# A layer-norm, graph-message, convolution and gating kernel: a new clock for the planner that orders its instructions

## The chip, the cores and the metric

The kernel runs on one core of a Trainium2 chip. The core has a matrix engine (TensorE, written PE in the profile, with PEld for its weight loads), a vector engine (VectorE, DVE), an activation engine (ScalarE, ACT), a general engine (GpSimd, POOL) and a queue engine (SyncE, SP). Each works through its own list of instructions in order and waits on semaphores for the others. DMA transfers are issued from SP, POOL and ACT. The metric is the device time of one execution in microseconds (us), lower is better. A measurement of this kernel can tell a difference of about 0.3%, some 6 us.

## The reference

The input is `x`, 32 batches of 512 nodes with 256 features, and `adj`, a 512 by 512 mask for each batch; everything is fp32. With `h = relu(layernorm(x))` the output is `x + gru(...)`:

```python
xc = transpose(h); c = relu(bn1(conv1(xc, 1 tap)))
x_conv = relu(bn2(conv2(c, 17 taps)) + xc)
s = h @ w_se.T + b_se                      # 3 numbers for each node
A = exp(-|s_n - s_m|^2) * adj
x_nmp = A @ relu(h @ w_msg.T + b_msg)
x_in = concat([x_conv, x_nmp])
gi = x_in @ w_ih.T + b_ih;  gh = h @ w_hh.T + b_hh
r = sigmoid(gi_r + gh_r); z = sigmoid(gi_z + gh_z)
out = x + (1 - z) * tanh(gi_n + r * gh_n) + z * h
```

## The kernel before

**The work.** The 32 batches pass through five parts, and each part is a Python generator, called a stream, that emits instructions and now and then yields.

- `begins` (`begin`) turns a normalised batch into the layout with features on partitions (`hT`), on PE and ACT for the first 8 batches and with VectorE transposes after a trip through DRAM (`xd`) for the others, and stores it to DRAM (`hd`).
- `rows` (`all_rows`, `rows`, `conv1`) loads `hT` back (`load_row`, two buffers shared with `begins`) and makes the 1-tap convolution into `h1`, the input of the 17-tap convolution.
- `conv` (`convolution`) computes the 17-tap convolution with a scheme of transformed operands and weights: 7 groups of batches, 25 products in each. VectorE prepares the operands (`operand_some`), VectorE and ACT prepare the 25 transformed weights during group 0 (`prepare_some`), which are stored to `wd` and loaded again for later groups (`load_weights`). After a product ACT copies the PSUM banks out (`z`, `n`), VectorE sums them into `y`, and `evacuate` (L711) scales `y` on ACT into `part`, a ring of two buffers, from which POOL stores to `cd`. For the first two batches it writes `xconv` directly.
- `graphs` (`graph`) loads `hTg`, makes messages, the four small products and exponentials of the kernel matrix (`kernel_exp`), masks them (`masked`) and multiplies (`gather`). The small products use one bank of the convolution (`pair[1]`) and three banks of the pool `ps_g`.
- `gates` (`gates`, `unit`) computes the gated unit and stores to `out` with accumulating DMAs from POOL. Its large weights lie in a pool `late` that takes the room of the weight preparation's pool `prep` (`late_pools`).

**What sets the order.** The order of instructions on every engine is fixed while the program is built, by a planner with a simulated clock. `now` is PE's clock: each matmul adds its cost (`matmul`, L134). The `Engine` class (L116) keeps for VectorE and ACT the time at which each would be free. The loop at the end of the kernel takes, of the streams whose last yielded time is not after `now`, the one with the lowest pacing clock, lets it emit up to its next yield, and calls `fill()` (L1530), which runs due actions from the list `LATER`, `evacuate`, and background work (norms, operands, weights, sums) while VectorE is planned to be free within 1.5 us. The stream `rows` has the lowest pacing clock, so it goes first whenever it is ready. If no stream is ready, `now` advances by 0.25.

**The clock before.** An `Engine` operation starts at `max(self.free, now)` and takes `fixed + each * size`; it knows nothing of what its operands wait for. A consumer is held until `free + LAG`, with `LAG = 0.6`. DMAs are issued directly and their landing is a guess, such as `HR_AT[b] = now + 8.0` in `load_row` and `PARTS.append(act.free + 5.0)` in `evacuate`. PE's clock never waits for an operand or a bank. Loads enter SP's list where the planner emits them; on the chip SP waits there until the buffer is free, and whatever stands behind it waits too.

Of the kernel before, what the change touches and what calls it, by code (L numbers as in the profile page):

```python
# [50 lines left out]
def kernel(  # L51
# [43 lines left out]
    const = ctx.enter_context(tc.tile_pool(name="const", bufs=1))  # L95
    front = ctx.enter_context(tc.tile_pool(name="front", bufs=2))
    cv = ctx.enter_context(tc.tile_pool(name="cv", bufs=1))
    dram = ctx.enter_context(tc.tile_pool(name="dram", bufs=1, space=bass.MemoryType.DRAM))
    acc = ctx.enter_context(tc.tile_pool(name="acc", bufs=3, space=PSUM))
    gps = ctx.enter_context(tc.tile_pool(name="gps", bufs=3, space=PSUM))  # L100
    first_ctx = ExitStack()
    cps = first_ctx.enter_context(tc.tile_pool(name="cps", bufs=2, space=PSUM))
    ctx.enter_context(tc.manual_schedule())
    late = None

    now = 5.0
    LAG = 0.6
# [6 lines left out]

    class Engine:
        def __init__(self, engine, fixed, each):
            self.engine, self.fixed, self.each, self.free = engine, fixed, each, 0.0

        def behind(self, other):
            self.free = max(self.free, other.free + 0.1)

        def __getattr__(self, name):
            def issue(*tiles, **more):
                size = max(elements(t) for t in tiles if hasattr(t, "shape"))
                self.free = max(self.free, now) + self.fixed + self.each * size
                getattr(self.engine, name)(*tiles, **more)  # L128

            return issue  # L130

    dve, act = Engine(nc.vector, 0.12, 0.00108), Engine(nc.scalar, 0.16, 0.0009)

    def matmul(ps, lhsT, rhs, **more):  # L134
        nonlocal now
        now += max(0.223, 0.005 + elements(ps) / 600.0)
        nc.tensor.matmul(ps, lhsT, rhs, **more)  # L137

    def turn(ps, a):
        nonlocal now  # L140
        now += 0.11
        nc.tensor.transpose(ps, a, ident)  # L142

    def keep_warm(n):

        for _ in range(n):
            nc.tensor.transpose(unused[:, :P], ident, ident)
# [22 lines left out]
    def store_at(t, dst, src):  # L170
        todo = [lambda: nc.gpsimd.dma_start(dst, src)]

        def run():
            if todo:
                todo.pop()()

        STORES.append(run)
        later(t, run)
# [8 lines left out]
    ARRIVES = (0.0, 7.0, 11.0, 13.0)  # L187
# [6 lines left out]
    def fetch(b, xs=None):  # L194
        XS[b] = front.tile([P, NT, D], F32, name="x_sb", bufs=2) if xs is None else xs
        step = NT // 2 if b == 0 else NT
        for c in range(0, NT, step):
            nc.sync.dma_start(
                XS[b][:, c : c + step], x[b].rearrange("(c p) d -> p c d", p=P)[:, c : c + step]
            )  # L200

    def load(b, xs=None):
        if b not in XS:
            fetch(b, xs)
        NORMS[b] = norm(b)
        NORM_AT[b] = max(now + 7.0, 50.0) if b >= G else ARRIVES[b]

    def load_row(b):
        if b not in HR:
            settle_stores()  # L210
            HR[b] = front.tile([P, ND, N], F32, name="hT", bufs=2)
            nc.sync.dma_start(HR[b], HD[b])
            HR_AT[b] = now + 8.0

    def load_graph(b):
        if b < B and b not in HG and begun > b:
            settle_stores()
            HG[b] = front.tile([P, ND, N], F32, name="hTg", bufs=1)
            nc.sync.dma_start(HG[b], HD[b])

    def load_gates(b):
        if b >= B or b in HB:
            return
        settle_stores()
        HB[b] = late.tile([P, ND, N], F32, name="hTb", bufs=2)
        nc.sync.dma_start(HB[b], HD[b])
        HB_AT[b] = now + 8.0

    def load_conv(b):

        if b < B and b not in XC and evacuated.get(b, 1e9) <= now:
            XC[b] = late.tile([P, ND, N], F32, name="xconv", bufs=2)
            nc.sync.dma_start(XC[b], CD[b])
            XC_AT[b] = now + 7.0
# [14 lines left out]
    def load_sums(b, d):  # L249
        if b < B and (b, d) not in XN:  # L250
            settle_stores()
            XN[b, d] = late.tile([P, N], F32, name="xnb", bufs=2)
            nc.sync.dma_start(XN[b, d], ND_[b, d])
            XN_AT[b] = now + 6.0
# [3 lines left out]
    vec = const.tile([P, _NCOL], F32)  # L258
    nc.sync.dma_start(vec, vecs)
    w1 = const.tile([P, ND, D], F32)  # L260
    nc.sync.dma_start(w1, conv1_w)

    prep_ctx = ExitStack()
    prep = prep_ctx.enter_context(tc.tile_pool(name="prep", bufs=1))
    wraw = prep.tile([P, ND, 2, 3, 3, D], F32)
    nc.gpsimd.memset(wraw[:, :, 0, 0, 0, :], 0.0)
# [3 lines left out]
    wmsg = const.tile([P, ND, D + 3], F32)  # L270
    bmsg = const.tile([P, D + 3], F32)
    ident = const.tile([P, P], F32)
    make_identity(nc, ident)
    mhalf = const.tile([P, 4], F32)
    nc.gpsimd.memset(mhalf, -0.5)

    def rsqrt(dst, var):
# [4 lines left out]
        nc.gpsimd.tensor_tensor(dst, t[:, :n], mhalf[:, :n], op=ALU.pow)  # L282
# [15 lines left out]
    h1 = const.tile([P, Q * RV], F32)  # L298
# [4 lines left out]
    def zeros(g):  # L303
        at = input_of(g)
        for b in range(B + 1):
            v = U * b - STARTS[g]
            if 0 <= v <= sizes(g)[0]:
                nc.gpsimd.memset(at[:, : Q if v == sizes(g)[0] else LEAD, :, v : v + 1], 0.0)
                if v > 0:
                    nc.gpsimd.memset(at[:, Q - 1 : Q, :, v - 1 : v], 0.0)  # L310
# [3 lines left out]
    class Graphs:  # L314


        def __init__(self):
# [6 lines left out]
            nc.gpsimd.memset(self.aug, 1.0)  # L324
            nc.gpsimd.memset(self.augr, 0.0)
            nc.gpsimd.memset(self.augl, -1.0)
# [3 lines left out]
        def ask(self, more):  # L330
# [3 lines left out]
            for k in range(self.asked, min(self.asked + more, NT * B)):  # L334
# [3 lines left out]
                if b < TURNED:  # L338
                    nc.sync.dma_start(m, adj[b, c * P : (c + 1) * P, :])
                for g in range(P // 32 if b >= TURNED else 0):  # L340
                    at = c * P + 32 * g
                    nc.sync.dma_start(
# [37 lines left out]
    def norm_some(b):  # L380

        if now < NORM_AT[b]:
            return False
# [152 lines left out]
    def weights_first():  # L536
# [10 lines left out]
        for j1 in ORDER:  # L547
# [12 lines left out]
            for j2 in ORDER:  # L560
# [7 lines left out]
                for k in range(2):  # L568
# [4 lines left out]
                    nc.scalar.dma_start(WD[len(WS)][:, k], w[k])  # L573
# [4 lines left out]
    def weights_again():  # L578


        for m in range(25, 25 * NG):
            W_BASE.append(taken)
            w = {}
            for k in (1,) if m % 25 == LONE else (2, 0, 1):
                yield
                w[k] = new_w()
                if k < 2 or m >= 50:
                    nc.sync.dma_start(w[k], WD[m % 25][:, k])
            WS.append(w)
            W_AT.append(now + 7.0)  # L590
# [10 lines left out]
    def third_weight(m):  # L601
# [5 lines left out]
        later(dve.free + 0.4, lambda: nc.gpsimd.dma_start(WD[m % 25][:, 2], w[2]))  # L607
# [103 lines left out]
    def evacuate():  # L711
# [10 lines left out]
        if g == 0 and b < 2:  # L722
# [10 lines left out]
            if o == ND - 1:  # L733
                evacuated[b] = XC_AT[b] = act.free + 0.7 + LAG
# [7 lines left out]
        act.free += 0.7  # L742
        PARTS.append(act.free + 5.0)
        n0, n1 = Q * first, min(Q * last, N)
        later(act.free + 0.4, lambda: nc.gpsimd.dma_start(CD[b][:, o, n0:n1], part[:, : n1 - n0]))
        if o == ND - 1 and last == U:
            evacuated[b] = PARTS[-1]
# [34 lines left out]
    def prepare_some():  # L782
        nonlocal prepare_at
        if len(WS) >= 25 or len(WS) >= at_product + 3 or now < prepare_at:
# [4 lines left out]
    def convolution():  # L789
# [28 lines left out]
        for g in range(NG):  # L818
# [3 lines left out]
            if g == 1:  # L822
                first_ctx.close()
                cps = ctx.enter_context(tc.tile_pool(name="cps2", bufs=1, space=PSUM))
# [3 lines left out]
            for n in range(25):  # L828
# [6 lines left out]
                if late is None and len(WS) >= 25:  # L835
# [48 lines left out]
    def late_pools():  # L884
        nonlocal late, wih, whh, wsum, tsum
        prep_ctx.close()
        late = ctx.enter_context(tc.tile_pool(name="late", bufs=1))
        whh = late.tile([P, ND, 3 * D], F32, name="whh")
        wih = late.tile([P, 2 * ND, 3 * D], F32, name="wih")
        nc.sync.dma_start(whh, w_hh)  # L890
        nc.sync.dma_start(wih, w_ih)
# [80 lines left out]
    def kernel_exp(at):  # L972

        nonlocal now, bank_at, exp_waits
# [6 lines left out]
        for c in range(NT):  # L981
            k = slice(32 * c, 32 * c + 5)
            nc.tensor.matmul(  # L983
# [3 lines left out]
        now += 1.15  # L987
# [33 lines left out]
    def blocks(t, rows, o):  # L1021
        for g in range(P // 32):
            at = o * P + 32 * g
            nc.sync.dma_start(
# [11 lines left out]
    def begin(b):  # L1036
# [4 lines left out]
        if b >= TURNED:  # L1041
# [3 lines left out]
            nc.gpsimd.dma_start(XD_[b].rearrange("(c p) d -> p c d", p=P), xs)  # L1045
            yield now + 7.0
# [3 lines left out]
            yield now + 8.0  # L1050
# [8 lines left out]
            nc.gpsimd.dma_start(HD[b], HT[b])  # L1059
# [9 lines left out]
        for d in range(ND):  # L1069
            norm_t(b, d)  # L1070
# [6 lines left out]
    def rows(g, b):  # L1077
        nonlocal made, made_at
        for o in range(ND):
            conv1(g, b, o)  # L1080
# [5 lines left out]
    def graph(b):  # L1086
# [3 lines left out]
        if b == 0:  # L1090
            HG[0] = HT[0]
            yield act.free + LAG
        elif b not in HG:
            load_graph(b)
            yield now + 9.0
        msg = front.tile([P, NT, D], F32, name="msg", bufs=1)
        for c in range(NT):
            messages(b, msg, c)
            yield now
        told = b + 1  # L1100
        factors()
        yield dve.free + LAG
# [11 lines left out]
        for n in range(NT):  # L1114
            masked(b, at, n)
# [4 lines left out]
        for d in range(ND):  # L1120
            gather(b, msg, at, d)
# [4 lines left out]
    def gates(b):  # L1126
# [4 lines left out]
        if b < B - 1:  # L1131
            nc.sync.dma_start(out[b], x[b])
        else:
            nc.sync.dma_start(out[b][:, :P], x[b][:, :P])
# [3 lines left out]
        if b == 0:  # L1138
            yield now + 8.0
# [70 lines left out]
        def store(y, o, s):  # L1210
            for g in range(P // 32):
# [3 lines left out]
                if is_last(o):  # L1215
                    (nc.scalar if g % 2 else nc.sync).dma_start(dst, src)
                else:
                    nc.gpsimd.dma_start(dst, src, accum_op=ALU.add)  # L1218

        fast = FIRST_FAST <= b < B - PLAIN  # L1220
        if b == B - PLAIN:
            for w, at in ((whh, w_hh), (wih, w_ih)):
                nc.sync.dma_start(w[:, 0, D : 2 * D], at[:, 0, D : 2 * D])
# [331 lines left out]
    def all_rows():  # L1555
# [5 lines left out]
        for g in range(1, NG):  # L1561
            for b in batches(g):
# [5 lines left out]
                rows_wait = True  # L1568
                load_row(b)
                if b + 1 in batches(g) and b + 1 < begun:  # L1570
                    later(now + 2.5, lambda b=b: load_row(b + 1))
# [25 lines left out]
    unused, waits = acc.tile([P, N], F32, name="ps_acc"), 0  # L1597
    keep_warm(16)
# [7 lines left out]
    brz = const.tile([P, 2 * ND], F32)  # L1606
# [6 lines left out]
    bn = const.tile([P, ND], F32)  # L1613
# [9 lines left out]
    nc.sync.dma_start(wmsg[:, :, :D], w_msg)  # L1623
    nc.sync.dma_start(wmsg[:, :, D:], w_se)
    nc.sync.dma_start(bmsg[:, :D], b_msg.to_broadcast([P, D]))
    nc.sync.dma_start(bmsg[:, D:], b_se.rearrange("k o -> o k").to_broadcast([P, 3]))
    for c in range(ND):
        for k0, k1 in ((0, 9), (9, TAPS)):
            nc.sync.dma_start(wflat[:, c, k0 + 1 : k1 + 1, :], conv2_w[:, c, k0:k1, :])
# [78 lines left out]
```

## Time and profile before

| | |
|---|---|
| median of 3 runs | 2067.28 us (2066.85 to 2071.51) |
| profiled execution's own time | 2067.35 us |
| span of its instructions | 2065.6 us |
| PE busy | 2012.4 us, 97% of the span |
| DVE, ACT, POOL busy | 69%, 43%, 22% |
| mean granted TensorE clock | 0.989 of full |
| DMA engines, mean over slices from 0.4 to 0.98 | 183 GB/s |

The profiled execution is 0.07 us over the median, and 1.8 us of it lie outside the span. A wait row reads: engine, what it wanted to do, `<-`, what released it, then total us, how often, and the longest. In the window rows the columns are the stretch, its length, and then the busy time and the number of instructions of PE, PEld, DVE, ACT and POOL, the granted clock, the DMA share and GB/s. In a timeline row: start, duration, engine, line, operation, output and inputs, count, and in brackets the idle time of the engine before it with its releaser. Most operations stand at the line of a helper (L128, L137, L142), so that tile names tell them apart.

### The profile page before, as it was taken

What the parts mean: (1) busy time and instruction counts of PE and PEld (TensorE: products, weight loads), DVE (VectorE), ACT (ScalarE), POOL (GpSimd) and SP (SyncE); (2) the same over time, 40 slices, a digit from 0 to 9 for tenths busy, and PEclk for the clock granted to TensorE, in tenths of its full rate; (3) what the DMA queues carried; (4) which work ended last, traced back from release to release, by engine and by line L of the source; (5) the groups of instructions that cost most, each with busy time, mean ns of one, the idle gap of its engine ahead of it and who ended that gap; (6) DMA issues with size and microseconds to landing.
All of it is one profiled execution on the core that took longest, in us unless ns stands there. A gap on an engine that the chain in (4) does not pass through costs nothing. (4 is left out here: it accounts for less than half of the span.)

```text
span 2065.6 us, 27386 instructions
## 1 busy us (share of the span) xinstructions
PE 2012.4 (97%) x9199; PEld 1360.9 (66%) x9199; DVE 1416.3 (69%) x2626; ACT 888.4 (43%) x1805; POOL 451.1 (22%) x578
## 2 busy tenths in 40 slices
PE   8999889999999999999999999999999999999998
PEld 4878556676676766677577676667775677664444
DVE  6789378885878848687587775677875777752223
ACT  6554454335543445433454334554334633334221
POOL 2101022321212213122141221231221311114222
PEclk9999999999999999999999999999999999999999
DMA  7455668898979869778789788797886776756554
GB/s 286 150 174 184 225 209 196 192 226 226 223 197 203 190 192 205 201 182 212 183 193 223 172 204 206 164 197 204 207 204 175 189 158 159 173 118 143 63 92 36
DMA packets 581227, 378.70 MB, mean 183 GB/s; under 512 B 457648, under 2 KB 475344, under 8 KB 579952
## 3 DMA queue, kind: packets, MB, share of 16 engines
q1 hardware_dynamic: 419616, 279.02, 49.1%
q0 software_dynamic: 153184, 84.70, 23.9%
q10 hardware_dynamic: 8288, 13.24, 1.7%
q8 instruction: 73, 1.20, 0.2%
q14 instruction: 66, 0.54, 0.1%
HBM read 278.81 MB, written 114.56 MB: 190 GB/s over the span
## 5 line engine op out<-in xcount | busy, mean ns | idle before, releaser
L1218 POOL DMA_DIRECT2D out_dram<-o_sb x252 | 275.9, 1718 | 659.1 <-DVE o_sb L128 628.9
L137 PE MATMUL ps_acc<-xnb,wih 128*128 128x512 f32 (+1 forms) x772 | 364.4, 593 | 0.7 <-DVE ps_acc L128 0.7
L137 PEld LDWEIGHTS ps_c<-xd,w 128*128 128x128 f32 x2304 | 288.6, 191 | 55.0 <-issue 38.9
L137 PEld LDWEIGHTS ps_c<-x,w 128*128 128x128 f32 x2032 | 258.4, 193 | 72.3 <-issue 49.2
L137 PE MATMUL ps_c<-xd,w 128*128 128x135 f32 (+1 forms) x2304 | 291.8, 280 | 7.0 <-ACT ps_c L128 7.0
L137 PE MATMUL ps_c<-x,w 128*128 128x135 f32 (+2 forms) x2032 | 267.4, 281 | 11.4 <-ACT n L128 5.0
L137 PE MATMUL ps_acc<-hTb,whh 128*128 128x512 f32 (+2 forms) x580 | 239.5, 523 | 0.4 <-ACT r L128 0.4
L137 PE MATMUL ps_acc<-xconv,wih 128*128 128x512 f32 (+1 forms) x580 | 238.9, 519 | 0.3 <-DVE ps_acc L128 0.3
L137 PE MATMUL ps_g<-at,msg 128*128 128x512 f32 x512 | 227.1, 593 | 0.8 <-DVE at L128 0.8
L137 PEld LDWEIGHTS ps_acc<-xnb,wih 128*128 128x128 f32 x772 | 142.6, 191 | 115.6 <-issue 108.7
L137 PEld LDWEIGHTS ps_g<-at,msg 128*128 128x128 f32 x512 | 95.4, 190 | 106.4 <-issue 101.1
L137 PEld LDWEIGHTS ps_acc<-xconv,wih 128*128 128x128 f32 x580 | 107.6, 190 | 74.9 <-issue 67.5
L137 PEld LDWEIGHTS ps_acc<-hTb,whh 128*128 128x128 f32 x580 | 104.8, 191 | 78.6 <-issue 71.2
L128 DVE TENSOR_TENSOR msg<-ps_g,bmsg 128x256 f32<-128x256 f32 x128 | 53.7, 420 | 143.5 <-PE ps_g L137 143.1
L128 DVE SCALAR_TENSOR_TENSOR x<-x,x 128x544 f32<-128x544 f32 (+5 forms) x161 | 137.5, 854 | 2.9
L128 DVE TENSOR_TENSOR o_sb<-hTb,r 128x512 f32<-128x512 f32 x63 | 43.3, 687 | 124.1 <-ACT r L128 123.5
L128 ACT ACTIVATE ps_c<-ps_c 128x270 f32<-128x270 f32 (+1 forms) x144 | 56.1, 389 | 167.8 <-PE ps_c L137 167.8
L128 DVE TENSOR_TENSOR x<-x 128x272 f32<-128x272 f32 (+5 forms) x280 | 127.4, 497 | 0.2
L137 PE MATMUL ps_g<-hT,w 128*128 128x512 f32 (+8 forms) x296 | 122.1, 560 | 3.7 <-DMA hT<-hd 2.5
L137 PE MATMUL ps_g<-wmsg,hTg 128*128 128x259 f32 x496 | 123.5, 382 | 0.7 <-DVE aug L128 0.7
L128 ACT ACTIVATE h<-ps_g,bn_shift,bn_scale 128x252 f32<-128x252 f32 (+8 forms) x212 | 86.5, 485 | 73.2 <-PE ps_g L137 73.2
L128 DVE TENSOR_TENSOR xd<-x 128x544 f32<-128x544 f32 (+1 forms) x144 | 102.5, 716 | 14.0 <-PE ps_c L137 13.7
(149 smaller groups left out, 2927.5 us busy)
## 6 DMA issues: line engine op xcount, KB each, us to landing
w<-wd SPq DMA_DIRECT2D x414, 256.0 KB, 3.4
m_sb<-in_adj_dram SPq DMA_DIRECT2D x384, 64.0 KB, 3.8
hT<-hd SPq DMA_DIRECT2D x33, 512.0 KB, 4.4
hd<-hT POOLq DMA_DIRECT2D x32, 512.0 KB, 5.5
hTb<-hd SPq DMA_DIRECT2D x32, 512.0 KB, 4.6
xnb<-nd SPq DMA_DIRECT2D x64, 256.0 KB, 3.0
out_dram<-o_sb POOLq DMA_DIRECT2D x252, 64.0 KB, 4.9
hTg<-hd SPq DMA_DIRECT2D x31, 512.0 KB, 4.3
```

The source lines that it names most:

```text
L128: getattr(self.engine, name)(*tiles, **more)
L137: nc.tensor.matmul(ps, lhsT, rhs, **more)
L1218: nc.gpsimd.dma_start(dst, src, accum_op=ALU.add)
```

## The change

Only the planner changes; the arithmetic, the tiles, the pools' sizes and the number of matmuls of the computation stay. All instructions may come in another order.

1. **Dependencies in the clock.** Every tile's reads and writes are noted by region (`region`, `note`). An operation starts at `max(self.free, after(...))`, where `after` gives the end of the writes of its inputs and of all accesses to its output, plus `HAND = 0.04` across engines, and the release of the ring buffer under it (`BORN`). PE's `now` waits in the same way (`on_pe`).
2. **Durations.** The constants are replaced: VectorE 0.12 + 0.00108 per element becomes 0.066 + 0.00106 plus a tail of 0.085; ACT 0.16 + 0.0009 becomes 0.05 + 0.00087 plus a tail of 0.12, with a factor of 2.2 for outputs whose last step is over 8 elements and 0.1 for each bias or scale tile. `LAG` becomes 0.17.
3. **DMAs in the clock.** `sp`, `pool` and `act` issue DMAs through `Engine.dma_start`, with an issue time, 8 transfers in flight for the hardware queues and 8 for POOL's, and a common line (`FLOW`) of 1.85 us and a rate. Its result replaces the guesses: `HR_AT`, `HB_AT`, `XC_AT`, `XN_AT`, `W_AT` and `NORM_AT` become `done(...)`, and `PARTS` gets the modelled end of the store to `cd`.
4. **Loads and buffers.** `load_row` is asked for when the ring `hT` is to be free (0.5 earlier), the transposes of `begin` wait for `front.free("hT", 2)`, and the streams yield until `gps.free("ps_g")` before they take a bank.
5. **A gate on ACT.** `norm_some` and `prepare_some` return at once when ACT is planned busy for more than `BUSY = 0.5` beyond `now`. `late_pools` waits until `prep.over() <= now + 1.0`.

```diff
-    LAG = 0.6
+    LAG = 0.17
+    BUSY = 0.5
+    HAND = 0.04
...
+    def after(who, outs, ins):
+        at = 0.0
+        for a in ins:
+            for k, end in met(a.tensor.name, region(a)):
+                if k[4]:
+                    at = max(at, end if k[5] == who else end + HAND)
+        for a in outs:
+            at = max(at, BORN.get(a.tensor.name, 0.0))
+            for k, end in met(a.tensor.name, region(a)):
+                if k[5] != who:
+                    at = max(at, end + HAND)
+        return at
...
+        def free(self, name, bufs=None):
+            ring, n = self.rings.get(name, []), bufs or self.bufs
+            return released(ring[-n]) + HAND if len(ring) >= n else 0.0
...
+        def dma_start(self, dst, src, **more):
+            run = 4 * min(dst.ap[-1][1], src.ap[-1][1])
+            name = "P" if self.name == "POOL" else "H"
+            lanes = LANES.setdefault(name, [0.0] * 8)
+            at = max(self.free, after("DMA", [dst], [src]), lanes[0])
+            if name == "P":
+                issue = 1.1 if run < 512 else 0.78 if run == 1024 else 0.55
+            else:
+                issue = 0.53 if run < 512 else 0.43 if run == 1024 else 0.37
+            self.free = at + issue
+            rate = 150e3 if run < 512 else 330e3
+            flow = (self.free + 1.85, 4 * elements(dst) * dst.shape[0] / rate)
+            FLOW.append(flow)
...
+            for arrives, cost in FLOW:
+                end = max(end, arrives) + cost
+                if (arrives, cost) == flow:
+                    break
...
-                size = max(elements(t) for t in tiles if hasattr(t, "shape"))
-                self.free = max(self.free, now) + self.fixed + self.each * size
+                at = max(self.free, after(self.name, some[:1], some[1:] + given))
+                wide = some[0].ap[-1][0] > 8 and self.name == "ACT"
+                each = self.each * (2.2 if wide else 1.0)
...
+                self.free = at + fixed + each * max(elements(t) for t in some) + 0.1 * len(given)
+                note(self.name, some[:1], some[1:] + given, self.free + self.tail)
...
-    dve, act = Engine(nc.vector, 0.12, 0.00108), Engine(nc.scalar, 0.16, 0.0009)
+    dve, act = Engine("DVE", nc.vector, 0.066, 0.00106, 0.085), Engine("ACT", nc.scalar, 0.05, 0.00087, 0.12)
...
+    def on_pe(out, ins, took):
+        nonlocal now
+        now = max(now, after("PE", [out], ins)) + took
+        note("PE", [out], ins, now + 0.163)
...
-            HR_AT[b] = now + 8.0
+            HR_AT[b] = done(HR[b])
...
-        if now < NORM_AT[b]:
+        if now < NORM_AT[b] or act.free > now + BUSY:
             return False
...
-        act.free += 0.7
-        PARTS.append(act.free + 5.0)
+        PARTS.append(1e9)
+        mine = len(PARTS) - 1
...
+        def leaves():
+            PARTS[mine] = pool.dma_start(CD[b][:, o, n0:n1], part[:, : n1 - n0])
+            if o == ND - 1 and last == U:
+                evacuated[b] = PARTS[mine]
+
+        later(act.free + 0.2, leaves)
...
-        if len(WS) >= 25 or len(WS) >= at_product + 3 or now < prepare_at:
+        if len(WS) >= 25 or len(WS) >= at_product + 3 or now < prepare_at or act.free > now + BUSY:
...
-                if late is None and len(WS) >= 25:
+                if late is None and len(WS) >= 25 and prep.over() <= now + 1.0:
                     late_pools()
...
+            yield gps.free("ps_g")
             messages(b, msg, c)
...
+                yield front.free("hT", 2) - 0.5
                 load_row(b)
```

## The prediction

> **What bounds the kernel now.** I read the page's first lines, then who PE waited for, then the busy time by stretches, then the timeline at the two longest groups of pauses, and last the DMA rows.
>
> ```profile
> span 2065.6 us, 27386 instructions
> PE 2012.4 (97%) x9199; PEld 1360.9 (66%) x9199; DVE 1416.3 (69%) x2626; ACT 888.4 (43%) x1805; POOL 451.1 (22%) x578
> PEclk9999999999999999999999999999999999999999
> ```
>
> PE is the bound almost everywhere, and its work does not change. So all that a new order can win is PE's idle time, 2065.6 - 2012.4 = 53.2 us, and the time lost while its clock was lowered: the mean granted clock is 0.989, so 1.1% of 2065.6, about 23 us. At the end 6.5 us follow PE's last matmul (2059.1); 46.7 us of idle lie ahead of it. The wait rows over the whole span add up to nearly that:
>
> ```profile
> PE ps_c L137 <- ACT ps_c L128: 7.0, 5, 3.1
> PE ps_c L983 <- ACT z L128: 6.7, 3, 4.0
> PE ps_c L137 <- ACT n L128: 5.0, 5, 2.0
> PE ps_c L137 <- ACT z L128: 4.4, 3, 1.7
> PE ps_g L137 <- DMA hT<-hd: 2.5, 2, 1.2
> ```
>
> The reader is to see that PE waits for ACT, few times and long, and hardly for a load. Asked for by stretch, the waits before 280 us sum to 27.4 us and those after to 18.8 us; of the first, 5.0 lie before 30 us, the start. Where the pauses stand, the clock falls:
>
> ```profile
> 206.00:222.00 16.00, 12.37 (x43) 6.04 (x42) 9.12 (x21) 6.73 (x16) 1.30 (x1) 0.79 0.27 97
> 269.00:280.00 11.00, 6.13 (x47) 5.39 (x46) 10.59 (x16) 10.46 (x16) 2.90 (x5) 1.00 0.73 233
> 564.00:578.00 14.00, 9.19 (x45) 8.15 (x44) 13.76 (x24) 7.38 (x13) 7.38 (x9) 0.76 1.09 230
> 834.00:850.00 16.00, 11.99 (x47) 7.42 (x46) 12.05 (x18) 11.39 (x18) 6.31 (x6) 0.79 0.61 92
> ```
>
> The timeline shows two causes. First, evacuation:
>
> ```profile
> 564.35 1.37 ACT L128 ACTIVATE part<-y,bn_shift,bn_scale 128x522 f32<-128x522 f32 x1
> 567.19 1.20 PE L137 MATMUL ps_c<-x,w 128*128 128x136 f32 x8 [1.74 <-ACT z L128]
> 567.27 1.38 ACT L128 ACTIVATE part<-y,bn_shift,bn_scale 128x522 f32<-128x522 f32 x1
> 570.11 1.02 ACT L128 ACTIVATE part<-y,bn_shift,bn_scale 128x360 f32<-128x360 f32 x1 [1.45 <-DMA cd<-part]
> 570.93 0.48 ACT L128 ACTIVATE ps_c<-ps_c 128x272 f32<-128x272 f32 x1
> 571.46 0.82 PE L137 MATMUL ps_c<-xd,w 128*128 128x136 f32 x2 [3.07 <-ACT ps_c L128]
> ```
>
> At 570.11 ACT stands for 1.45 us because `part`'s old contents had not landed, and the bank copy that PE needs is queued behind. Second, the small products at 842 us:
>
> ```profile
> 837.17 4.43 ACT L128 ACTIVATE y<-z 128x1620 f32<-128x1620 f32 x3
> 841.63 0.68 ACT L128 ACTIVATE z<-ps_c 128x270 f32<-128x270 f32 x2
> 842.37 1.22 PE L983 MATMUL ps_c<-right,left 5*128 5x512 f32 x1 [4.01 <-ACT z L128]
> ```
>
> **The idle time in five heaps.** Evacuation: 2.0 + 2.9 us at 273 and 277 and 1.7 + 3.1 at 567 and 571, together 9.7. Small products behind `z`: 6.7. Loads of `hT`: 2.5. The start: 5.0. The rest of the head, 30 to 280 us: 27.4 - 5.0 - 4.9 = 17.5. The rest after 280: 18.8 - 4.8 - 6.7 - 2.5 = 4.8. The clock by slices of 52 us (0.93 is 3.6 us lost, 0.97 is 1.6): 0 to 52 us 3.6; 52 to 155 3.1; 207 to 310 7.2; 568 to 620 3.6; 826 to 878 3.6; the rest under 3.
>
> **Durations and evacuation.** The planner before gives a `part` of 522 elements 0.16 + 0.0009 x 522 + 0.7 = 1.33; the row says 1.34, so that was right. But the same shape written to `xconv` in group 0 it gives 0.61 where the row says 1.31: over four large ones 2.8 us of ACT work that it doesn't see, and PE's 4.9 us near 275 follow them. The new clock gives 0.05 + 2.2 x 0.00087 x 504 + 0.2 + tail = 1.33. For `part` the guess is the landing: act.free + 5, where the stores issued at L745 took 3.6 us in the median and up to 9.0, and POOL can be busy first with 4.4 us of output stores. ACT stood 12.7 us, 16 times, for these landings. With `PARTS` at the modelled landing, and unknown until the store is issued, `evacuate` steps aside. Of 9.7 us I take 8.4 away; the cover is that the other streams then have PE work, which 97% busy supports. The clock loss at 568 (3.6) goes with it: -12. If `part` is late next, `xconv` loads and the gates are later, but they are asked for far ahead (no PE wait for `xconv` now).
>
> **A rule on the clock.** The row: the 16 us at 206 ran at 0.79 after pauses of 2.5 and 1.1 us, with three matmuls between. [...]
>
> **The gate on ACT and the head.** Norms and weight preparation no longer pile up on ACT when it is 0.5 us behind. In the head PE waits for `n`, `z`, `w`, `right` and `augr`, single waits of up to 2.5 us, from ACT half busy and DVE 75 to 93% busy in the 52 us slices from 52 to 207. What DVE limits stays. No row shows how much of the 17.5 us is order and how much is work; the ends are 0 and 17.5, and I take half, 8.7, since DVE is idle for 17 us at 250 while PE still waits. Half of the clock loss from 52 to 310 (10.3) goes too: -5. The gate's own price is a late weight; PE's wait for `w` is 2.2 us now and `prepare_some` stays up to 3 weights ahead, which hides it. Without that cover 25 weights at 1 us each would cost 25 us. `late_pools` moved by a product or two: 24 matmuls of 0.11 each, 2.7 us, of gates' start, paid nowhere because gates' work is only put off among other PE work.
>
> **The small products.** The three copies take 4.43 us; the planner before already gives 3 x 1.62. `kernel_exp` yields for `bank_at` only when a product is open, and that is unchanged. The 6.7 us may fall elsewhere: 0, with ends -10 (its clock loss with it) and +10.
>
> **Loads and their queue.** Asking for `hT` when its buffer is free takes SP's waits at L212 (57 us for stores, 48 for conv1's matmuls) off SP; behind them stood weights, masks and the other copies of `hT`. PE hardly waited for those, so this wins the 2.5 us at most. Against it stands the missing margin: before, a row was held for 8 us after the ask; now until the modelled landing, and `rows` goes first when ready, so a late landing is a pause of PE. For 512 KB the empty line gives 0.37 + 1.85 + 1.59 = 3.81 us.
>
> ```profile
> hT<-hd SPq DMA_DIRECT2D x33, 512.0 KB, 4.4
> q1 hardware_dynamic: 419616, 279.02, 49.1%
> q0 software_dynamic: 153184, 84.70, 23.9%
> ```
>
> The median is 4.4, one in ten takes over 6.6. `FLOW` adds what was planned ahead, in one line by arrival. [...] By the row it is 0.6 at the median, 33 x 0.6 = 20 us, before `FLOW`'s own addition and the emission step (0.9 to 3.4 us of matmuls), which swallow most. I take 0.15 us each, near the row: +5. The other loads (`hTg`, `hTb`, `xnb`, weights) are asked for a stage ahead. Nor does the wait for `ps_g` add work; PE's waits for that pool's banks were a few us.
>
> **Margins.** `LAG` falls from 0.6 to 0.17 and durations lose their padding: an ACT copy of 272 is 0.05 + 0.24 + 0.12 = 0.41 against the row's 0.40; VectorE's 128x512 is 0.69 against 0.69. An error of 0.05 us now shows. With some 60 places where PE has nothing else, 3 us; ends 0 and 10.
>
> **Sum.** -12 (evacuation) - 13.7 (head) - 2.5 + 5 (loads) + 3 (margins) = -20.2. From the profiled execution's 2067.35, which is the median's 2067.28, to 2047.
>
> **Rivals.**
> *Nearly all pauses go.* The clock now sees what PE waited for. Idle 9.7 + 17.5 + 2.5 + 6.7 and the clock in 52 to 310, 568 and 826 (17.5) are 54 us; with four fifths of it 2024. Against it: the copies of `y` and VectorE's load in the head are work, not order. Chance 0.19.
> *The stalls move.* Every order has its own collisions on ACT, and from 880 us on the old guesses left PE over 99% busy to the end of the convolution; the slow places are a few accidents that the new order replaces by others. Then 2061 to 2073, 2067. This is also the case in which the new waits change little. Chance 0.11.
> *Just in time is too late.* Place: PE ahead of `conv1`, behind `hT<-hd`. Without loads the sum is -22.7; it turns at 22.7 / 33 = 0.7 us lateness of a mean load. At 1 us it is +33, and two pauses that drop the clock add 7: 2084. For it: the 4.4 against 3.81, DMA shares of 0.8 to 0.97 from 310 to 720 us. Against it: only 2.5 us were waited for `hT` so far. Chance 0.26.
>
> **How the numbers follow.** The forecast, 2036 to 2060, has 0.44. Faster by over 0.3% (a run of this kernel tells about that from no change, 6 us): 0.44 + 0.19 = 0.63; same 0.11; slower 0.26. The range leaves out the best two fifths of the first rival (0.08) and the worst two fifths of the last (0.11): 2021 to 2087. The forecast's own range is 2036 to 2060.
>
> **What would show it.** Right: PE's waits for `n` and `ps_c` near 275 and 570 gone, ACT's wait for `cd<-part` well under 12.7, granted clock over 0.99, SP's waits at `load_row` near zero. The forecast is wrong if PE's row `<- DMA hT<-hd` exceeds 10 us, if waits for `w` or `x` grow (the gate starves preparation), or if the count of idle-time transposes at L147 (41 now) rises much, which means that the planner itself found nothing to do.

## The result, and the profile after

The changed kernel took 2058.1 us in the median of 5 runs (2053.89 to 2060.96) against 2067.28 (2065.06 to 2071.51) before: the ratio is 0.9948, interval 0.9929 to 0.9967. That is 9 us faster, inside the forecast range and less than half of the 20 us forecast. The profiled execution took 2055.33 us with a span of 2053.6, 12.0 us shorter than the span before.

The first lines of the page of the changed kernel:

```profile
span 2053.6 us, 27368 instructions
PE 2008.7 (98%) x9203; PEld 1353.0 (66%) x9203; DVE 1418.0 (69%) x2626; ACT 887.6 (43%) x1785; POOL 448.8 (22%) x578
```

The 12.0 us divide into PE's idle time, which fell from 53.2 to 44.9 (8.3), and its busy time, which fell from 2012.4 to 2008.7 (3.7). The clock gave more than the second part: the mean granted clock rose from 0.989 to 0.994, and laid over PE's busy time the lowered clock cost 20.4 us before and 11.4 after, 9.0 less. So, apart from the clock, PE was busy some 5 us longer. Of this, four more idle-time transposes (45 with 11.3 us, from 41 with 9.5) are at most 1.8 us; the rest is spread over many kinds of matmuls and was not explained. Where in the span? The busy time by stretches, first the kernel before, then the changed one:

```profile
0.00:280.00 280.00, 252.31 (x1432) 187.91 (x1433) 201.15 (x438) 149.63 (x325) 35.48 (x73) 0.95 0.58 202
280.00:1850.00 1570.00, 1550.98 (x7270) 1079.20 (x7269) 1150.61 (x2102) 683.56 (x1407) 352.70 (x442) 0.99 0.81 194
```

```profile
0.00:280.00 280.00, 263.44 (x1499) 196.52 (x1500) 208.99 (x449) 156.79 (x336) 36.19 (x76) 0.97 0.60 210
280.00:1850.00 1570.00, 1548.20 (x7236) 1068.02 (x7235) 1156.64 (x2102) 680.75 (x1382) 351.45 (x442) 1.00 0.81 193
```

In the same first 280 us PE now issues 67 more matmul records, at 0.97 of the clock instead of 0.95. From 280 to 1850 us it is no busier than before. PE's waits say the same: between 30 and 280 us they sum to 11.0 us, from 22.4; after 280 us to 21.5 us, from 18.8. The clock does not change that: in the first 280 us idle time and lowered clock together cost 16 us less, after them 1 us less. So the net gain comes from the head.

The waits of PE in the changed kernel from 280 us on:

```profile
PE ps_c L259 <- ACT z L241: 6.5, 4, 3.8
PE ps_c L259 <- ACT ps_c L241: 4.6, 9, 1.2
PE ps_g L259 <- DMA hT<-hd: 4.1, 5, 1.5
PE ps_acc L259 <- DVE ps_acc L241: 3.0, 5, 1.5
```

The reader is to see more waits than before (29 in all, from 20), and shorter ones. The long one, 3.8 us, has a new cause. The timeline of the changed kernel there:

```profile
343.76 0.69 DVE L241 TENSOR_TENSOR w<-w 128x512 f32<-128x512 f32 x1 [5.59 <-DMA w<-wd]
346.22 0.42 DVE L241 TENSOR_TENSOR msg<-ps_g,bmsg 128x256 f32<-128x256 f32 x1
346.67 0.63 ACT L241 ACTIVATE msg<-msg 128x512 f32<-128x512 f32 x1 [9.43 <-DVE msg L241]
347.21 0.66 ACT L241 ACTIVATE z<-ps_c 128x272 f32<-128x272 f32 x2
347.64 0.76 PE L259 MATMUL ps_c<-x,w 128*128 128x136 f32 x2 [3.80 <-ACT z L241]
```

VectorE stands 5.6 us for a weight load that the planner took for landed. Behind it, after an operand's preparation (1.93 us, not shown), is a message, behind the message an ACT operation, behind that the copy of the bank that PE wants. So here a load that lands late, with 5.59 us of VectorE's time, is seen as PE waiting 3.80 us for ACT. VectorE's waits for DMAs in the two kernels, before first:

```profile
DVE xconv L128 <- DMA xconv<-cd: 26.2, 9, 6.4
DVE w L128 <- DMA w<-wd: 7.8, 2, 5.2
```

```profile
DVE xconv L241 <- DMA xconv<-cd: 46.2, 15, 12.6
DVE w L241 <- DMA w<-wd: 22.1, 7, 6.2
```

### The profile page after: what moved, and what is told of

Read it like the earlier page. It is cut to its first block, busy times and chain, and to the rows that moved or that the text cites. A ratio compares the mean times of both kernels' runs of the same rounds, so it can differ in the third digit from the quotient of the medians.

```text
span 2053.6 us, 27368 instructions
## 1 busy us (share of the span) xinstructions
PE 2008.7 (98%) x9203; PEld 1353.0 (66%) x9203; DVE 1418.0 (69%) x2626; ACT 887.6 (43%) x1785; POOL 448.8 (22%) x578
## 5 line engine op out<-in xcount | busy, mean ns | idle before, releaser
L259 PEld LDWEIGHTS ps_g<-wmsg,hTg 128*128 128x128 f32 x496 | 91.1, 190 | 27.0 <-issue 16.3
```

## Experiments

### Is the gain the new clock's, or this order's?

A small edit of a pacing constant has no merit of its own, but it gives another order. Two edits of this kind were made to each kernel.

```diff
 # b_nudge_gates (kernel before)
-        "gates": (all_gates(), 31.25 * PER, 1.8),
+        "gates": (all_gates(), 31.25 * PER, 1.82),
 # b_nudge_graphs (kernel before) and a_nudge_graphs1 (changed kernel)
-        "graphs": (all_graphs(), 11.5 * PER, -0.5),
+        "graphs": (all_graphs(), 11.5 * PER, -0.48),
 # a_nudge_graphs2 (changed kernel)
-        "graphs": (all_graphs(), 11.5 * PER, -0.5),
+        "graphs": (all_graphs(), 11.5 * PER, -0.52),
```

> The kernel before with the pacing start of the gates stream at 1.82 instead of 1.8: an edit without a meaning of its own, which gives another order. Theory A (the new clock removes pauses by seeing their causes): the old clock gives much the same pauses in any order, 2063 to 2072 us. Theory B (an order is a draw, and the change drew a better one): 2050 to 2085, with pauses of PE in other places and 5 us or more away from 2067.

> The kernel before with the pacing start of the graphs stream at -0.48 instead of -0.5. Theory A: 2063 to 2072 us. Theory B: 5 us or more away from 2067, on either side.

> The changed kernel with the pacing start of the graphs stream at -0.48 instead of -0.5. Theory A: 2054 to 2062 us, PE's waits after 280 us between 17 and 26 us. Theory B: 2045 to 2075, and no nearer to 2058 than the nudged kernels before are to 2067.

> The changed kernel with the pacing start of the graphs stream at -0.52 instead of -0.5. Theory A: 2054 to 2062 us. Theory B: 2045 to 2075.

| kernel | median us | ratio to before (interval) | PE's waits 30 to 280 us | after 280 us | clock |
|---|---|---|---|---|---|
| before | 2067.28 | 1 | 22.4 | 18.8 | 0.989 |
| b_nudge_gates | 2075.75 | 1.0034 (1.0022 to 1.0046) | 22.3 | 23.1 | 0.985 |
| b_nudge_graphs | 2065.83 | 0.9982 (0.9969 to 0.9995) | 17.5 | 18.5 | 0.988 |
| changed | 2058.10 | 0.9948 (0.9929 to 0.9967) | 11.0 | 21.5 | 0.994 |
| a_nudge_graphs1 | 2060.50 | 0.9955 (0.9939 to 0.9972) | 11.2 | 23.2 | 0.992 |
| a_nudge_graphs2 | 2092.79 | 1.0114 (1.0092 to 1.0136) | 20.7 | 33.3 | 0.987 |

A step of 0.02 in one constant moves the changed kernel by 35 us, four times the whole gain, and the kernel before by up to 8. The slow one has pauses everywhere, the head too: its largest waits there are for VectorE's `at` (4.5 us) and `augr` (3.9), where the changed kernel has 0.2 and 2.1. Neither theory had all four right: b_nudge_graphs and a_nudge_graphs1 came out as theory A said, b_nudge_gates as theory B said, and a_nudge_graphs2 lies outside both. What it shows is the heart of theory B: a step without meaning can cost more than the change gains, so an order is in part a draw. The means of the three orders under each clock are nearly equal (2069.6 before and nudged, 2070.5 changed and nudged), with spreads of 10 and 35 us, so nothing here shows that the new clock gives better orders on the whole. The changed kernel's own order is one of the good ones.

One row is no draw of the head: by the order of operations in the traces b_nudge_gates does what the kernel before does until some 590 us, which is why both have the same waits there. Of the others, b_nudge_graphs departs from its parent near 140 us and the two nudges of the changed kernel near 75.

### One duration mended in the old clock

```diff
 # b_wide (kernel before)
+                wide = self.fixed == 0.16 and tiles[0].ap[-1][0] > 8
-                self.free = max(self.free, now) + self.fixed + self.each * size
+                self.free = max(self.free, now) + self.fixed + self.each * size + (0.7 if wide else 0.0)
...
-        act.free += 0.7
```

> The kernel before with one duration mended: 0.7 us added in the planner's ACT clock for every write with a last step over 8 elements, so the evacuations into xconv of group 0 are counted in full (those into part had it already). Evacuation theory: PE's waits near 275 us (4.9 us for n and ps_c) go, and 2062 us. Rival (the head's gain comes from the waits of operations in the clock, not from durations): the waits only move, 2067 plus or minus 4.

Measured: 2077.44 us, ratio 1.0036 (1.0021 to 1.0052). PE's waits between 262 and 285 us, in the kernel before and then in b_wide:

```profile
PE ps_c L137 <- ACT ps_c L128: 2.9, 1, 2.9
PE ps_c L137 <- ACT n L128: 2.0, 1, 2.0
```

```profile
PE ps_c L983 <- ACT n L129: 1.3, 1, 1.3
PE ps_c L138 <- ACT ps_c L129: 0.5, 1, 0.5
```

The planner now does what it was meant to do: where the kernel before has ACT write the eight pieces of `xconv` in two runs of four, 2.79 and 2.82 us long, b_wide has four pairs of some 1.45 us. The pauses named do shrink, 4.9 to 1.8 us, and those of the head from 22.4 to 14.2. That the mended duration did it is supported, not shown. In b_nudge_graphs, where nothing was mended and ACT writes all eight pieces in one run of 5.49 us, these two rows sum to 0.6 us between 262 and 285 us; a wait for `w` of 2.5 us stands there instead. And after 280 us b_wide's waits grow from 18.8 to 29.3, so the kernel is slower, outside what either theory said. The time is set by the other pauses, which are drawn anew.

### Edits of the changed kernel as a whole

```diff
 # a_land3
-                    at = max(at, end + HAND)
+                    at = max(at, end + HAND + (3.0 if k[5] == "DMA" else 0.0))
 # a_nogate
-    BUSY = 0.5
+    BUSY = 1e9
 # a_lag025
-    LAG = 0.17
+    LAG = 0.25
```

The first is in `done`.

> The changed kernel with 3 us added to every landing that the planner hands to the streams (done() of a tile written by a DMA); nothing else. Late-landing theory: VectorE's waits for w<-wd (22.1 us) and xconv<-cd (46.2 us) and PE's for hT (4.1 us) fall to under a third, PE's waits after 280 us fall from 21.5 to 10 to 15 us, and the time to 2046 to 2052. Rival (thin margins of ACT and VectorE durations make the small waits): the DMA waits fall, PE's waits after 280 us stay over 18 us, 2056 to 2062.

> The changed kernel without the gate on ACT (BUSY at 1e9, so norms and weight preparation are emitted however far ACT is behind). Gate theory: PE's waits between 30 and 280 us rise from 11 to 18 us or more, and 2064 to 2070. Rival (the head's gain comes from the clock alone): within 4 us of 2058.

> The changed kernel with LAG at 0.25 instead of 0.17, so each consumer of an ACT or VectorE result is held 0.08 us longer. Thin-margin theory: the nine waits of PE for the copy of the first bank (ps_c, 4.6 us) fall to half and the time by 2 to 5 us. Rival: no wait of that kind changes beyond what a nudge of the order does, 2054 to 2062.

Measured: a_land3 2082.24 us (ratio 1.0067, 1.0048 to 1.0086), a_nogate 2095.9 (1.013, 1.0113 to 1.0148), a_lag025 2078.65 (1.0044, 1.0028 to 1.0061). All three are slower than before, and all three times lie outside what was expected under either theory; none lies outside what a nudge does (2092.79), or hardly. In a_land3 VectorE's waits for weights fell from 22.1 to 2.3 us, as the late-landing theory had it, and for `xconv` from 46.2 to 16.9, nearly so; PE's wait for `hT` hardly fell (3.6 us, from 4.1), and PE's waits rose to 20.3 in the head and 27.2 after it: other pauses. In a_nogate the head's waits are 23.3 us, as the gate theory had it; since a_nudge_graphs2 has 20.7 with the gate, this proves nothing about the gate. In a_lag025 the waits for the first bank's copy did not fall (6.3 us, from 4.6). Each is inconclusive on its cause, because each departs from the changed kernel's order within the first 40 us. One thing a_lag025 does show: its head is nearly as good as the changed kernel's (12.6 us of waits), yet with 36.0 us after it the kernel is slower than before. A good head alone is not enough.

### The head held, the rest drawn anew

The next edits act only from a planner's clock of 300 on, so the order of the head stays the changed kernel's. Two add time to landings, two are their controls.

```diff
 # a_late_land15 and a_late_land30, in done
-                    at = max(at, end + HAND)
+                    at = max(at, end + HAND + (1.5 if k[5] == "DMA" and now > 300.0 else 0.0))
...
+                    at = max(at, end + HAND + (3.0 if k[5] == "DMA" and now > 300.0 else 0.0))
 # a_late_nudge_up and a_late_nudge_down, in the last loop
+        if now > 300.0 and not nudged:
+            nudged, clock["graphs"] = True, clock["graphs"] + 0.02
...
+            nudged, clock["graphs"] = True, clock["graphs"] - 0.02
```

> The changed kernel with 1.5 us added to every landing handed to the streams, only from a planner's clock of 300 on; the order of the head is the changed kernel's. Late-landing theory: PE's waits before 280 us stay at 16 us, VectorE's waits for w<-wd (22.1 us) and xconv<-cd (46.2 us) fall to under half, PE's waits after 280 us fall from 21.5 to under 15, and 2048 to 2053 us. Draw theory (any edit gives another order, whose pauses are as many): the VectorE waits fall, PE's waits after 280 us are 20 to 35 us, and 2056 to 2080.

> The same with 3 us. Late-landing theory: VectorE's waits for both loads under a quarter, PE's for hT near 0, 2046 to 2052 us. Draw theory: 2056 to 2080, with no order between this run and the one with 1.5 us.

> The changed kernel with the pacing clock of the graphs stream set 0.02 later, once, at a planner's clock of 300: the control of the two runs with later landings, with the same head. Draw theory: 2052 to 2075 us, PE's waits after 280 us between 20 and 33. If the changed planner itself makes the pauses few (accuracy theory): 2056 to 2061, waits within 4 us of 21.5.

> The same with the clock set 0.02 earlier. Draw theory: 2052 to 2075 us, and not the same as its twin. Accuracy theory: 2056 to 2061.

| kernel | median us | ratio to before (interval) | PE's waits 30 to 280 us | after 280 us | VectorE for `w`, `xconv` | PE for `hT` |
|---|---|---|---|---|---|---|
| changed | 2058.10 | 0.9948 (0.9929 to 0.9967) | 11.0 | 21.5 | 22.1, 46.2 | 4.1 |
| a_late_land15 | 2053.38 | 0.9925 (0.9900 to 0.9949) | 10.5 | 17.1 | 3.4, 52.0 | 0.5 |
| a_late_land30 | 2061.17 | 0.9961 (0.9947 to 0.9976) | 11.1 | 24.1 | 2.4, 41.6 | 2.6 |
| a_late_nudge_up | 2052.68 | 0.9922 (0.9906 to 0.9939) | 10.4 | 19.7 | 21.6, 65.1 | 4.0 |
| a_late_nudge_down | 2060.79 | 0.9959 (0.9944 to 0.9974) | 11.7 | 26.6 | 19.5, 50.2 | 4.3 |

First, with the head held all five orders beat the kernel before, by 0.4 to 0.8%, and PE's waits in the head stay at 10.4 to 11.7 us, while those after it, 17.1 to 26.6 us, are on the whole no fewer than before (18.8): the gain of these five lies in the head's order. Of the theories, draw had the controls' times right; a_late_land15 fits neither, and neither theory expected `xconv` to stay.

Second, VectorE's waits for weights fell where landings were made later, to 3.4 and 2.4 us, and did not in the controls. The rows of a_late_land15, and then of a_late_nudge_up:

```profile
DVE w L241 <- DMA w<-wd: 3.4, 3, 1.6
```

```profile
DVE w L241 <- DMA w<-wd: 21.6, 7, 6.4
```

That is what a margin of the landing would do, but the controls can't show it. By the order of operations in the traces a_late_nudge_down does what the changed kernel does until some 490 us, and a_late_nudge_up until some 540, while the two with later landings depart soon after 300. All waits for weights in the controls lie before 456 us, so the controls only repeat the changed kernel's own. An order that was redrawn earlier, without any margin, has few of them too. The row of a_nudge_graphs1:

```profile
DVE w L241 <- DMA w<-wd: 4.2, 3, 2.4
```

The three kernels with later landings have 2.3 to 3.4 us of these waits, the seven of the new clock without 4.2 to 26.1. So the margin is the likely cause, and a redraw that happens to avoid them is not excluded. The waits for `xconv` are not cured: 1.5 and 3 us more leave them, with single waits of 12 us, much as they were. And the time does not follow: 2053.4 and 2061.2 with later landings, 2052.7 and 2060.8 without. What a cured wait is worth is less than what the order draws. The two best orders, a_late_nudge_up and a_late_land15, also stand below the changed kernel's median, by 5 us; their intervals overlap with its own, so they are not shown to be faster than it.

## Why the prediction was right or wrong

**The bound** was right in the main: the gain is idle time and clock, less some 5 us by which PE was busy longer. The direction and the range were right. Of the 20 us forecast, 9 came.

**Evacuation, -12.** Both groups of pauses are gone from their places, as forecast. The rows of the changed kernel:

```profile
269.00:280.00 11.00, 11.00 (x65) 8.12 (x64) 8.23 (x13) 6.73 (x14) 2.37 (x4) 1.00 0.85 321
564.00:578.00 14.00, 14.00 (x90) 11.72 (x90) 13.72 (x33) 4.99 (x12) 0.00 (x0) 1.00 0.62 212
```

For `xconv` the step is supported by b_wide, with the doubt told there. The step on `part` failed, "With `PARTS` at the modelled landing ... `evacuate` steps aside". ACT's wait for `cd<-part` was 12.7 us before and 8.6 in the changed kernel, but 12.0 to 21.6 in the nine other orders of the new clock, as in those of the old one (12.7 to 30.4). The changed kernel still has the pattern, at 1039 us:

```profile
1039.11 0.42 ACT L241 ACTIVATE part<-y,bn_shift,bn_scale 128x18 f32<-128x18 f32 x1 [1.85 <-DMA cd<-part]
1039.43 0.38 ACT L241 ACTIVATE ps_c<-ps_c 128x270 f32<-128x270 f32 x1
1039.87 1.88 PE L259 MATMUL ps_c<-xd,w 128*128 128x135 f32 x14 [1.19 <-ACT ps_c L241]
```

This wait of 1.85 us says that the modelled landing of the store is early. It was not tested: the edits of the landings act in `done`, which `PARTS` does not go through.

**The head, -13.7.** The size was near. Waits fell by 11.4 us, but 4.9 of these are the pauses near 275 us that the forecast counts under evacuation; of the heap of 17.5 us 6.5 went, where 8.7 was forecast. Between 52 and 310 us the clock rose from 0.96 to 0.97, 3.4 us, where 5 was forecast. The reason, that the clock and the gate bring it about, is not shown: a_nudge_graphs2 has the clock and the gate, and 20.7 us of waits in its head.

**The small products, 0.** They took 6.7 us of PE's waits after `z` before and 0.2 in the changed kernel, and the stretch from 834 to 850 us, next to where the group now runs (830 us), rose from 0.79 to the full clock. The guard is unchanged, as the prediction says; the collision did not fall in this order. With 3.4 us of clock that makes some 10 us, put at nothing and within the stated ends. It is not all a draw: behind `z` or `n` the small products waited 0.2 to 7.4 us in the ten orders of the new clock, and 5.6 to 13.7 in the four of the old one. Which part of the change does that was not tested.

**Loads, +5.** The rival "just in time is too late" had the right kind of cause and looked at the wrong queue. PE's wait for `hT` rose by 1.6 us only. The lateness of 0.6 us that the prediction reckons with is the row's 4.4 less the modelled 3.81; in the changed kernel these loads land after 3.8 us in the median. What failed in this order is "The other loads (`hTg`, `hTb`, `xnb`, weights) are asked for a stage ahead": VectorE waited 14 us more for weights, and 3.8 us reached PE at once at 347 us. It also waited 20 us more for `xconv`, which the prediction had "asked for far ahead". Other orders differ: a_nudge_graphs1 has 4.2 us for weights, less than the kernel before (7.8). Also wrong was that SP's waits at `load_row` would go. Told apart by the load that follows, SP stood before the loads of `hT` 65.5 us for the stores `hd<-hT` and 47.5 for conv1's matmuls, from 56.5 and 47.6: asking for a load when the planner has its buffer free took neither away.

**Margins, +3.** PE's waits after 280 us became 29 from 20, and sum to 2.7 us more, which includes the loads. a_lag025 gave no sign that a wider `LAG` helps.

**The rule on the clock.** For the pauses near 206 us the reading of the row held: with them gone the stretch runs at 1.00 instead of 0.79. As a price for any pause of that length it was too simple, and "Where the pauses stand, the clock falls" is not so in its own second row: PE stood idle for 4.9 of the 11 us from 269 at a clock of 1.00. What the traces show of it is in the last section.

**The rivals.** "The stalls move" was given 0.11 and is what the runs show after 280 us: 18.8 us of waits became 21.5, at other places. Its reason, "every order has its own collisions", holds for the kernel as a whole: 2052.7 to 2092.8 us for four nudges of one constant. The sum treated each pause as a debt that an exact clock pays off, one by one; the term that it had too small was what another order costs by itself. After 280 us 4.8 us of evacuation and 6.5 of small products went, and 14.0 us of other waits came (21.5 less what was left of 18.8), where the sum had 8 for loads and margins.

**Luck.** A gain of some 10 us that was put at nothing set off part of the new waits. And the constant of a_nudge_graphs2, 0.02 away, would have put the same change at 2092.8 us, slower than before. That the total lies in the range is in part the luck of this order.

## What to carry to other kernels

Where a planner writes the order, measure first what a meaningless nudge of it does: here 2058 became 2093, so single edits of the planner, each tried once, tell nothing below some 2%. To test a cause, hold the order of everything ahead of it and give the edit a control that only redraws the rest; read the wait that the edit is aimed at, not the total. Then look in the traces where the control's order really departs: here it was after the waits in question, and the control could not answer. And when a guessed wait becomes a modelled one, look for the late arrivals in the queues of the engines behind it: here a late load, 5.59 us of VectorE's waiting, showed up several instructions later as PE waiting 3.80 us for ACT.

## What was not expected of the hardware

The clock did not follow the length of a pause: in the kernel before it was lowered behind the one of 2.49 us that ends at 210.65 us, and not behind the one of 2.87 us that ends at 277.39. The averages over 11 to 16 us, here and in the prediction, hide why. Taken piece by piece, the granted clock in all 14 traces is 1.00 or 0.50, nothing between, and it changes only on a grid of steps of 3.41 us; a piece at 0.50 lasts one to three steps. In the piece at 0.50 from 210.87 us of the kernel before, the 128x512 matmuls of `hT` took 1040 ns in the mean, and 600 in the 32 us at full clock behind it. A lowered step costs up to some 1.7 us of PE's work, an estimate: half of its 3.41. Some steps of the kernel before:

```profile
207.46:210.87 3.41, 0.92 (x11) 0.68 (x13) 3.31 (x9) 1.22 (x3) 0.00 (x0) 1.00 0.61 247
210.87:217.69 6.82, 5.68 (x13) 1.99 (x10) 4.35 (x11) 2.22 (x5) 1.30 (x1) 0.50 0.00 0
272.30:275.72 3.42, 1.64 (x12) 1.40 (x12) 3.42 (x7) 3.42 (x9) 1.29 (x2) 1.00 0.65 241
```

What differs in these rows is the idle time within one step. From 207.46 us PE stood idle for 2.49 us of a step, and the next two ran at 0.50. From 272.30 it stood for 1.78 us, in the step behind that for 1.67: more in all, but no step had as much, and the clock stayed.

The idle time alone does not account for every lowered step. In the changed kernel a step without any idle time is followed by a lowered one:

```profile
1224.96:1228.37 3.41, 3.41 (x9) 1.26 (x8) 3.41 (x3) 2.93 (x8) 0.00 (x0) 1.00 0.62 210
1228.37:1231.78 3.41, 3.41 (x5) 1.35 (x4) 2.30 (x5) 0.47 (x2) 0.00 (x0) 0.50 0.00 0
```

In 2.1 us of the first of these steps PE ran nothing but the small products, whose matmuls are `5*128` in their rows where the others here are `128*128`. Counted as idle, they part the steps of all 14 traces. Of the full-clock steps after a trace's first lowered one, 92 have 2.0 us or more of idle time and such matmuls together, and all 92 are followed by a lowered step. Of 7926 with under 1.2 us none is, and of the 150 between 22 are. In the traces of the kernel before and the changed one alone it is 11 of 11, none of 1146, and 2 of 21. By idle time alone 19 lowered steps would follow one with under 1.0 us, 4 of them in these two. Most groups of small products take 1.14 us (30 of the 32 in the changed kernel), less than the 1.2 us under which no step was followed by a lowered one; the one at 1224 us took 3.10. The limits are read off these traces, and no run was made to test them.
